# Cross-attention in two layers on one core: projections as four column tiles side by side

## The chip, the cores and the metric

One NeuronCore of a Trainium2 chip. The metric is the device time of one execution in microseconds. The engines named below are PE (TensorE: matrix products, with its loads of the stationary operand shown apart as PEld), DVE (VectorE), ACT (ScalarE), POOL (GpSimd) and SP (SyncE, which here only issues DMAs).

## The reference

Two cross-attention layers follow each other on x (32 sequences of 256 tokens, 320 channels) with one context (32 sequences of 77 tokens, 512 channels), 20 heads of 16 channels. With this context of 77 tokens the parts of the reference for other kinds of context are empty, and each layer comes to this:

```python
q = heads(x @ Wq); k = heads(ctx @ Wk); v = heads(ctx @ Wv)
p = softmax(q @ k.T / sqrt(16))
x = merge(p @ v) @ Wo + bo + x
```

Layer 0 makes x for layer 1; both read the same context, so keys and values of both layers can be made at any time. All numbers are fp32.

## The kernel before

Activations are kept with channels on partitions. Sequences go in pairs (NB = 2, 16 pairs), and a *unit* is one pair in one layer, 32 in all, ordered so that layer 0 runs AHEAD = 4 pairs in front of layer 1. The 320 channels are split into two full parts of 128 rows and a rest of 64; the rests of both sequences of a pair share one tile of 128 rows, so a unit has NG = 5 groups of 128 channel rows by 256 tokens: g = 0 to 3 are (part, sequence), g = 4 holds both rests. Every group is eight heads.

The steps of a unit, with what each runs on PE (stationary rows x columns, then elements streamed):

- keys_rest (L225): the last 64 key channels of both sequences, four tiles of 128x32 side by side, 77 elements, four steps of the contraction. keys (L242): the two full parts for both sequences at once, one tile of 128x128, 154 elements, four steps each.
- queries (L266, through project) and queries_rest (L275, through project_rest).
- project (L175) is used for Q and for the output. For parts t = 0, 1, contraction blocks kc = 0, 1 and sequences b = 0, 1 it runs a 128x128 tile over 256 tokens (L195). The last 64 input channels are a 64-row contraction (last_channels, L184): sequence 0 lies in rows 0 to 63 and sequence 1 in rows 64 to 127, each a tile of 64x128. Where last_channels stands is set by rest: before part 0 (rest = 0), between the parts (1), or at the end (2). Queries use u % 2, the output 0, the last unit 2.
- project_rest (L213): the last 64 output channels, four tiles of 128x32, three contraction steps.
- vals (L290): values for a chunk of 128 context tokens of a layer (not of a pair; 20 chunks a layer, the last of 32 tokens): tokens are the columns of the stationary operand, 128x128, and 320 elements are streamed.
- maxima (L326): four tiles of 32x128; DVE takes the maxima over keys (L334). turn (L343) transposes them, and eight small DMAs (L347) put them into rows of the queries.
- scores (L360): four tiles of 32x77, eight products for each group; ACT takes exp (L366).
- values (L409): products (L380), four tiles of 77x32 side by side; then DVE, POOL and DVE divide and transpose.
- finish (L430, project on the output weights) and finish_rest (L438); DVE adds bias and residual (L421).

All results of PE go through one pool of eight PSUM banks, one tag. The order of every engine's work is written out by hand (manual_schedule): each group of each unit has a slot, slots run one after another, and in a slot steps are issued in the order load, maxima, turn, scores, values, rest, full, last (L497). "rest" holds keys_rest, queries_rest and finish_rest; "full" holds keys and vals; "last" holds queries and finish. Values of two groups are made in every second slot. So nearly every slot on PE is maxima, then scores, then perhaps values, then one of the projection steps. Loads come on SP's queue.

Of the kernel before, what the change touches and what calls it, by code (L numbers as in the profile page):

```python
# [86 lines left out]
def xattn_kernel(ctx: ExitStack, tc: tile.TileContext, xT, cT, cP, weights, outT):  # L90
    nc = tc.nc
# [10 lines left out]
    def bank(name):  # L102
        return psum.tile([P, 512], F32, tag="bank", name=name)
# [45 lines left out]
    for i in range(2):  # L149
        m = const.tile([P, 2 * NG, 32], F32, name=f"max_{i}")  # L150
# [15 lines left out]

    st = [{} for _ in units]

    def of_group(x, g):

        if g < 4:
            return x[:, (g // 2) * NT + (g % 2) * S : (g // 2) * NT + (g % 2 + 1) * S]
        return x[:, 2 * NT : NX]

    def project(ps, w, w2, x, rest=0):  # L175

        def last_channels():  # L180
            for t in range(2):
                for b in range(NB):
                    r = slice(64 * b, 64 * b + 64)
                    nc.tensor.matmul(  # L184
                        ps[t][b][:, 0:S], w2[r, 0, t * P : (t + 1) * P], x[r, 2 * NT : NX],
                        start=(t >= rest), stop=(t < rest),
                    )

        for t in range(2):
            if t == rest:  # L190
                last_channels()
            for kc in range(2):
                for b in range(NB):
                    i = kc * NT + b * S
                    nc.tensor.matmul(  # L195
                        ps[t][b][:, 0:S], w[:, kc, t * P : (t + 1) * P], x[:, i : i + S],
                        start=(kc == 0 and t < rest), stop=(kc == 1 and t >= rest),
                    )
        if rest == 2:
            last_channels()  # L200
# [34 lines left out]
    def keys(u):  # L235
        p, layer = units[u]
        w, c_sb = w_sb[layer], cs[u]
        kT = st[u]["k"]
        for t in range(2):
            ps = bank(f"psk_{u}_{t}")  # L240
            for kc in range(NKA):
                nc.tensor.matmul(  # L242
                    ps[:, 0 : 2 * L],
                    w["k"][:, kc, t * P : (t + 1) * P],
                    c_sb[:, kc, :],
                    start=(kc == 0),
                    stop=(kc == NKA - 1),
                )
            nc.vector.tensor_tensor(  # L249
                kT[:, :, 2 * t : 2 * t + 2].rearrange("p e g k -> p e (g k)"),  # L250
                ps[:, 0 : 2 * L].unsqueeze(1).broadcast_to([P, 2, 2 * L]),
                masks.unsqueeze(2).broadcast_to([P, 2, 2 * L]),
                ALU.mult,
            )
        kM = st[u]["km"] = work.tile([P, 2, NG, L], F32, tag="kM", name=f"kM_{u}", bufs=3)
        for e in range(2):
            nc.gpsimd.tensor_scalar_add(kM[:, e], kT[:, e], less[:, e : e + 1])  # L257

    def queries(u):
        p, layer = units[u]  # L260
        w = w_sb[layer]
        q0, _ = st[u]["q"] = [
            work.tile([P, NX], F32, tag=f"q{e}", name=f"q{e}_{u}", bufs=3) for e in range(2)
        ]
        ps = [[bank(f"psq_{u}_{t}_{b}") for b in range(NB)] for t in range(2)]
        project(ps, w["q"], w["q2"], xs[p], rest=u % 2)  # L266
        for g in range(4):
            nc.scalar.copy(of_group(q0, g), ps[g // 2][g % 2][:, 0:S])  # L268

    def queries_rest(u):  # L270
        p, layer = units[u]
        w = w_sb[layer]
        q0, q1 = st[u]["q"]
        ps = bank(f"psq_{u}_2")
        project_rest(ps, w["q"], w["q22"], xs[p])  # L275
        nc.scalar.copy(of_group(q0, 4), ps[:, 0:S])
        nc.sync.dma_start(out=q1, in_=q0)
# [6 lines left out]
    def vals(layer, i):  # L284

        n = min(P, B * L - i * P)
        stage, c_sb = stages[layer][i % 2], cvs.pop((layer, i))
        ps = bank(f"psv_{layer}_{i}")
        for kc in range(NKA):
            nc.tensor.matmul(  # L290
                ps[:n, :C],
                c_sb[:, kc, :n],
                w_sb[layer]["v"][:, kc, :],
                start=(kc == 0),
                stop=(kc == NKA - 1),
            )
        nc.scalar.copy(
            stage[:n].rearrange("p r e a d -> p r (e a) d")[:, :, 0:4:3, :],
            ps[:n, :C].rearrange("p (r e d) -> p r e d", e=2, d=HD),
        )  # L300
# [18 lines left out]
    def maxima(u, g):  # L319
        q0, kT, mx = st[u]["q"][0], st[u]["k"], maxes[u % 2]  # L320
        q = of_group(q0, g)
        ps = [bank(f"psm_{u}_{g}_{j}") for j in range(4)]
        for c in range(S // P):
            for j in range(4):
                r = slice(32 * j, 32 * j + 32)
                nc.tensor.matmul(  # L326
                    ps[j][:, c * 2 * L : (c + 1) * 2 * L],
                    q[r, c * P : (c + 1) * P],
                    kT[r, :, g, :],
                    start=True,  # L330
                    stop=True,
                )
        for j in range(4):
            nc.vector.tensor_reduce(  # L334
                mx[:, 2 * g : 2 * g + 2, 2 * j : 2 * j + 2],
                ps[j][:, : 4 * L].rearrange("p (c e k) -> p c e k", e=2, k=L),
                AX.X,
                ALU.max,
            )
# [87 lines left out]
    def finish(u):  # L427
        w = w_sb[units[u][1]]
        ps = [[bank(f"psy_{u}_{t}_{b}") for b in range(NB)] for t in range(2)]
        project(ps, w["o"], w["o2"], st[u]["o"], rest=2 if u == NU - 1 else 0)  # L430
        for g in range(4):
            add(u, g, ps[g // 2][g % 2])
# [18 lines left out]
    for u, (p, layer) in enumerate(units):  # L451
# [5 lines left out]
        if u > 0:  # L457
            at(s - 12, "load", lambda u=u: load_context(u))
        at(s - 8 if odd else s - 9, "rest", lambda u=u: keys_rest(u))
        at(s - 7 if odd else s - 8 if u else s - 9, "full", lambda u=u: keys(u))  # L460
        at(s - 9, "last", lambda u=u: queries(u))
        need = range(p * NB * L // P, ((p + 1) * NB * L - 1) // P + 1)
        new = [i for i in need if i >= made[layer]]
        for i in need:
            when = s - 5 if odd else s - 6
            if len(new) == 2:
                when = s - 6 if i < new[1] else s - 5
            if i in new:
                at(when - 3, "load", lambda layer=layer, i=i: load_chunk(layer, i))
                at(when, "full", lambda layer=layer, i=i: vals(layer, i))  # L470
                made[layer] += 1
            at(when, "full", lambda u=u, i=i: place_vals(u, i))
# [124 lines left out]
```

## Time and profile before

| quantity | value |
|---|---|
| median of the 3 runs shown | 1009.54 us |
| all three | 1003.88, 1009.54, 1009.67 us |
| the profiled execution: its own time | 1003.92 us |
| the profiled execution: its span | 1002.1 us |
| granted TensorE clock, mean | 1.0 |

The page gives each group of instructions with its busy time and the mean of one. The groups on PE that matter here, with the tile (stationary rows * columns) and the elements streamed:

```profile
L360 PE MATMUL pss<-q,kM 32*77 32x256 f32 x2560 | 171.3, 375 | 1.9 <-DMA q<-mT 1.9
L380 PE MATMUL po<-pT,v 77*32 77x256 f32 x2560 | 155.9, 382 | 0.0
L195 PE MATMUL psq<-x,w 128*128 128x256 f32 x512 | 123.3, 389 | 0.0
L195 PE MATMUL psy<-oT,w 128*128 128x256 f32 x512 | 119.1, 386 | 0.0
L242 PE MATMUL psk<-c,w 128*128 128x154 f32 x512 | 77.6, 305 | 0.0
```

Each line has the program's line, the engine, the tile written and those read, the shape, the number of records, the busy time and the mean length of one record (ns), and the time that PE was idle just ahead of such records. A product of fp32 operands shows as two records, each with a load of its own. Matmuls are pipelined and their ends are modelled, so records overlap in the list. The order of time (timeline) lists blocks of like records by their start; the chain of waits follows the work that ended last back to its cause.

### The profile page before, as it was taken

What the parts mean: (1) busy time and instruction counts of PE and PEld (TensorE: products, weight loads), DVE (VectorE), ACT (ScalarE), POOL (GpSimd) and SP (SyncE); (2) the same over time, 40 slices, a digit from 0 to 9 for tenths busy, and PEclk for the clock granted to TensorE, in tenths of its full rate; (3) what the DMA queues carried; (4) which work ended last, traced back from release to release, by engine and by line L of the source; (5) the groups of instructions that cost most, each with busy time, mean ns of one, the idle gap of its engine ahead of it and who ended that gap; (6) DMA issues with size and microseconds to landing.
All of it is one profiled execution on the core that took longest, in us unless ns stands there. A gap on an engine that the chain in (4) does not pass through costs nothing.

```text
span 1002.1 us, 29771 instructions
## 1 busy us (share of the span) xinstructions
PE 989.1 (99%) x12608; PEld 695.4 (69%) x12608; DVE 587.9 (59%) x1380; ACT 420.7 (42%) x905; POOL 183.0 (18%) x236
## 2 busy tenths in 40 slices
PE   7999999999999999999999999999999999999998
PEld 5666776667776767767677676677666776676755
DVE  2456655566665666555666555665656666566664
ACT  1354434444444434444444444443543444443453
POOL 2111102111120111101111021111201112011111
PEclk9999999999999999999999999999999999999999
DMA  5541222221132311323113132121322212230012
GB/s 207 185 150 40 77 69 95 68 75 66 52 121 68 109 52 42 120 78 118 37 60 101 64 121 69 68 74 58 122 78 72 69 44 94 68 104 30 24 71 80
DMA packets 53894, 82.69 MB, mean 83 GB/s; under 512 B 15556, under 2 KB 35652, under 8 KB 53762
## 3 DMA queue, kind: packets, MB, share of 16 engines
q1 hardware_dynamic: 53330, 78.96, 23.7%
q8 instruction: 99, 1.62, 0.6%
q10 hardware_dynamic: 432, 1.84, 0.5%
q14 instruction: 33, 0.27, 0.1%
HBM read 35.39 MB, written 10.49 MB: 46 GB/s over the span
## 4 chain that ended last, share of the span: by engine, by line
PE 97%; DVE 1%; DMA 1%; SPq 0%; POOL 0%; issue 0%; POOLq 0%
PE po L380 15%; PE pss L360 14%; PE psq L195 12%; PE psy L195 12%; PE psm L326 12%; PE psv L290 9%; PE psk L242 7%; PE psy L213 4%; PE psq L213 4%; PE psy L184 3%; PE psq L184 3%; PE psk L225 2%; DVE max L334 1%; DMA w<-in_w_dram 0%; SPq L347 0%; DVE turned L392 0%
## 5 line engine op out<-in xcount | busy, mean ns | idle before, releaser
L366 ACT ACTIVATE pT<-pss 77x512 f32<-77x512 f32 x640 | 327.1, 592 | 357.8 <-PE pss L360 357.8
L334 DVE TENSOR_REDUCE max<-psm 128x4 f32<-128x308 f32 x640 | 261.4, 471 | 267.6 <-PE psm L326 267.6
L401 POOL TENSOR_TENSOR normal<-turned,inv 128x256 f32<-128x256 f32 x160 | 99.4, 621 | 542.0 <-DVE inv L396 542.0
L360 PE MATMUL pss<-q,kM 32*77 32x256 f32 x2560 | 171.3, 375 | 1.9 <-DMA q<-mT 1.9
L380 PE MATMUL po<-pT,v 77*32 77x256 f32 x2560 | 155.9, 382 | 0.0
L326 PE MATMUL psm<-kT,q 32*128 32x154 f32 x2560 | 130.4, 314 | 1.3 <-DVE max L334 0.8
L326 PEld LDWEIGHTS psm<-kT,q 32*128 32x128 f32 x2560 | 92.9, 183 | 55.8 <-issue 52.6
L257 POOL TENSOR_SCALAR kM<-kT,less 128x385 f32<-128x385 f32 x64 | 80.0, 1263 | 268.9 <-DVE kT L249 268.9
L380 PEld LDWEIGHTS po<-pT,v 77*32 77x32 f32 x2560 | 75.3, 109 | 71.7 <-DVE max L334 28.8
L392 DVE STREAM_TRANSPOSE turned<-po 128x512 f32<-128x512 f32 x160 | 109.5, 684 | 24.3 <-PE po L380 24.3
L195 PE MATMUL psq<-x,w 128*128 128x256 f32 x512 | 123.3, 389 | 0.0
L360 PEld LDWEIGHTS pss<-q,kM 32*77 32x77 f32 x2560 | 109.1, 141 | 15.4 <-issue 3.2
L195 PE MATMUL psy<-oT,w 128*128 128x256 f32 x512 | 119.1, 386 | 0.0
L195 PEld LDWEIGHTS psq<-x,w 128*128 128x128 f32 x512 | 93.3, 190 | 27.1 <-issue 10.8
L195 PEld LDWEIGHTS psy<-oT,w 128*128 128x128 f32 x512 | 94.6, 190 | 22.3 <-issue 10.3
L421 DVE SCALAR_TENSOR_TENSOR x<-psy,w,x 128x256 f32<-128x256 f32 x160 | 72.7, 476 | 43.9 <-PE psy L195 40.7
L290 PE MATMUL psv<-w,cv 128*128 128x320 f32 (+1 forms) x320 | 96.7, 445 | 0.8 <-DVE max L334 0.8
L414 DVE STREAM_TRANSPOSE oT<-normal 128x256 f32<-128x256 f32 x160 | 71.1, 445 | 34.4 <-POOL normal L401 34.4
L290 PEld LDWEIGHTS psv<-w,cv 128*128 128x128 f32 (+1 forms) x320 | 56.2, 185 | 35.9 <-DVE max L334 12.5
L268 ACT COPY q<-psq 128x256 f32<-128x256 f32 x128 | 46.1, 373 | 82.8 <-PE psq L195 70.2
L242 PEld LDWEIGHTS psk<-c,w 128*128 128x128 f32 x512 | 70.2, 193 | 11.6 <-DVE max L334 11.4
L242 PE MATMUL psk<-c,w 128*128 128x154 f32 x512 | 77.6, 305 | 0.0
(28 smaller groups left out, 446.3 us busy)
## 6 DMA issues: line engine op xcount, KB each, us to landing
q<-q SPq DMA_DIRECT2D x32, 640.0 KB
x<-in_xT_dram SPq DMA_DIRECT2D x16, 640.0 KB
c<-in_cP_dram SPq DMA_DIRECT2D x32, 308.0 KB
cv<-in_cT_dram SPq DMA_DIRECT2D x38, 256.0 KB
out_dram<-x SPq DMA_DIRECT2D x15, 640.0 KB
v<-stage SPq DMA_DIRECT2D x26, 192.5 KB
q<-mT SPq DMA_DIRECT2D x256, 5.0 KB
w<-in_w_dram ACTq DMA_DIRECT2D x2, 640.0 KB
```

What stands on the lines that cost most here:

```text
L195: nc.tensor.matmul(ps[t][b][:, 0:S], w[:, kc, t * P : (t + 1) * P], x[:, i : i + S], start=(kc == 0 and t < rest), stop=(kc == 1 and t >= ...
L213: nc.tensor.matmul(ps[r, 0:S], lhsT, rhs, start=(kc == 0), stop=(kc == 2))
L242: nc.tensor.matmul(ps[:, 0 : 2 * L], w["k"][:, kc, t * P : (t + 1) * P], c_sb[:, kc, :], start=(kc == 0), stop=(kc == NKA - 1),)
L257: nc.gpsimd.tensor_scalar_add(kM[:, e], kT[:, e], less[:, e : e + 1])
L290: nc.tensor.matmul(ps[:n, :C], c_sb[:, kc, :n], w_sb[layer]["v"][:, kc, :], start=(kc == 0), stop=(kc == NKA - 1),)
L326: nc.tensor.matmul(ps[j][:, c * 2 * L : (c + 1) * 2 * L], q[r, c * P : (c + 1) * P], kT[r, :, g, :], start=True, stop=True,)
L334: nc.vector.tensor_reduce(mx[:, 2 * g : 2 * g + 2, 2 * j : 2 * j + 2], ps[j][:, : 4 * L].rearrange("p (c e k) -> p c e k", e=2, k=L), AX.X ...
L360: nc.tensor.matmul(ps[j][:L, e * S : (e + 1) * S], kM[r, e, g, :], q[r, :], start=True, stop=True,)
L366: nc.scalar.activation(st[u]["p", g][j][:L], ps[j][:L], AF.Exp, scale=SCALE)
L380: nc.tensor.matmul(po[32 * j : 32 * j + 32, e * S : (e + 1) * S], vpad[:L, b, pair, e].rearrange("p a d -> p (a d)"), pT[j][:L, e * S : (e ...
L392: nc.vector.transpose(turned[:, 0 : 2 * S], po)
L401: nc.gpsimd.tensor_tensor(normal.rearrange("p q e d -> p e q d"), outs, inv.unsqueeze(3).broadcast_to([P, 2, S // 32, HD]), ALU.mult,)
```

## The change

A helper by_columns cuts a product's output into slices of 32 rows and issues one product for each, with the same streamed operand and 32 columns of the stationary one. It is put in place of the single product at four places: the 64-row part of project (L184), the 128-row part of project (L195), keys (L242) and vals (L290). A 128x128 tile becomes four tiles of 128x32 side by side, the form that products and project_rest have; the pair of 64x128 tiles becomes eight tiles of 64x32. Slots, the order of steps, tiles and DMAs are as before. Lines below the helper move down by six.

```diff
@@ -166,6 +167,11 @@
 
     st = [{} for _ in units]
 
+    def by_columns(out, lhsT, rhs, **flags):
+
+        for m in range(0, out.shape[0], 32):
+            nc.tensor.matmul(out[m : m + 32], lhsT[:, m : m + 32], rhs, **flags)
+
     def of_group(x, g):
 
         if g < 4:
@@ -181,7 +187,7 @@
             for t in range(2):
                 for b in range(NB):
                     r = slice(64 * b, 64 * b + 64)
-                    nc.tensor.matmul(
+                    by_columns(
                         ps[t][b][:, 0:S], w2[r, 0, t * P : (t + 1) * P], x[r, 2 * NT : NX],
                         start=(t >= rest), stop=(t < rest),
                     )
@@ -192,7 +198,7 @@
             for kc in range(2):
                 for b in range(NB):
                     i = kc * NT + b * S
-                    nc.tensor.matmul(
+                    by_columns(
                         ps[t][b][:, 0:S], w[:, kc, t * P : (t + 1) * P], x[:, i : i + S],
                         start=(kc == 0 and t < rest), stop=(kc == 1 and t >= rest),
                     )
@@ -239,7 +245,7 @@
         for t in range(2):
             ps = bank(f"psk_{u}_{t}")
             for kc in range(NKA):
-                nc.tensor.matmul(
+                by_columns(
                     ps[:, 0 : 2 * L],
                     w["k"][:, kc, t * P : (t + 1) * P],
                     c_sb[:, kc, :],
@@ -287,7 +293,7 @@
         stage, c_sb = stages[layer][i % 2], cvs.pop((layer, i))
         ps = bank(f"psv_{layer}_{i}")
         for kc in range(NKA):
-            nc.tensor.matmul(
+            by_columns(
                 ps[:n, :C],
                 c_sb[:, kc, :n],
                 w_sb[layer]["v"][:, kc, :],
```

## The prediction

> **What bounds the kernel now.** I read the page first: busy shares, then the chain that ended last, then the waits of PE, then the order of time of PE in a steady stretch.
>
> ```profile
> span 1002.1 us, 29771 instructions
> PE 989.1 (99%) x12608; PEld 695.4 (69%) x12608; DVE 587.9 (59%) x1380; ACT 420.7 (42%) x905; POOL 183.0 (18%) x236
> PE 97%; DVE 1%; DMA 1%; SPq 0%; POOL 0%; issue 0%; POOLq 0%
> ```
>
> ```profile
> PE psk L225 <- DMA w<-in_w_dram: 5.7, 1, 5.7
> PE pss L360 <- DMA q<-mT: 1.9, 2, 1.6
> ```
>
> PE is busy all the time, the chain runs through PE for 97% of the span, and the waits of PE for others come to some 10 us, 5.7 of them at the start. So a nanosecond saved on PE is a nanosecond saved, and the question is what PE's time consists of. The order of time shows it (first column: start; second: first start to last modelled end, so I use the distance to the next line's start instead):
>
> ```profile
> 500.04 1.99 PE L195 MATMUL psq<-x,w 128*128 128x256 f32 x8
> 501.96 1.14 PE L184 MATMUL psq<-x,w 64*128 64x256 f32 x8
> 503.03 1.99 PE L195 MATMUL psq<-x,w 128*128 128x256 f32 x8
> 504.95 0.81 PE L326 MATMUL psm<-kT,q 32*128 32x154 f32 x16
> 505.58 1.04 PE L360 MATMUL pss<-q,kM 32*77 32x256 f32 x16
> 506.55 1.93 PE L380 MATMUL po<-pT,v 77*32 77x256 f32 x32
> 508.31 0.72 PE L225 MATMUL psk<-c,w 128*32 128x77 f32 x32
> 508.95 1.13 PE L184 MATMUL psy<-oT,w 64*128 64x256 f32 x8
> 510.02 3.72 PE L195 MATMUL psy<-oT,w 128*128 128x256 f32 x16
> 513.67 0.81 PE L326 MATMUL psm<-kT,q 32*128 32x154 f32 x16
> 514.30 1.10 PE L360 MATMUL pss<-q,kM 32*77 32x256 f32 x16
> 515.33 2.37 PE L242 MATMUL psk<-c,w 128*128 128x154 f32 x16
> 517.63 0.81 PE L326 MATMUL psm<-kT,q 32*128 32x154 f32 x16
> ...
> 521.03 1.48 PE L213 MATMUL psy<-oT,w 128*32 128x256 f32 x24
> 522.33 1.48 PE L213 MATMUL psq<-x,w 128*32 128x256 f32 x24
> 523.74 0.81 PE L326 MATMUL psm<-kT,q 32*128 32x154 f32 x16
> 524.37 1.04 PE L360 MATMUL pss<-q,kM 32*77 32x256 f32 x16
> 525.34 2.42 PE L290 MATMUL psv<-w,cv 128*128 128x320 f32 x8
> 527.69 0.81 PE L326 MATMUL psm<-kT,q 32*128 32x154 f32 x16
> ```
>
> Every fp32 product is two records, so L195's 16 records are eight products.
>
> **A pass costs the same in both forms.** L195 takes 3.65 us for 16 records and 1.92 for 8: 1.73/8 = 0.216 us a record, plus 0.19 a block. L213 takes 1.30 for 24 records of four tiles side by side: 6 passes of 0.217, plus nothing, because the next block has the same form. Four tiles of 32 columns thus stream 256 elements as fast as one tile of 128 columns. L225 (77 elements) takes 0.64 - 0.11 (below) = 0.53 for 8 passes, 0.066 each, so four loads and four products can be issued every 0.066 us; the slimmest pass that the change makes has 154 elements. The change gains nothing inside a block. (The page's "mean ns of one" and busy time hide this, since each block's modelled tail is counted in.)
>
> **What is paid at a change of form.** L213 before another L213 takes 1.30, before L326 1.41: leaving a four-tile form costs 0.11. L380, entered from L360 and followed by L225 of its own form, takes 1.76 for 8 passes, 8 x 0.216 + 0.03: entering costs 0.03. A block of 128 columns pays 0.19 to 0.20 for both together (L195 0.19; L184 1.07 - 4 x 0.216 = 0.21; L242 and L290 likewise).
>
> **What the Trainium skill says.** *TensorEngine Tiling (Array Packing)*, Tiling Modes, Key Properties: changing the tiling mode, not just the tile, drains TensorE. The trace agrees, at 0.09 to 0.11 a change. L326 to L360 (0.63) shows no drain: 32x77 counts as 32x128. *TensorE: Matmul & The Clock Gate*, LDWEIGHTS (loading the stationary operand): a load takes about columns/1.2 ns and rows don't matter, so an estimate of 107 ns for 128 columns and 27 for 32. That is the entry: after a drain the load for the second record of a product lies open. The 0.03 of L380 agrees with 27; 0.19 splits into 0.107 entry and 0.09 exit; with L242's pass, (2.30 - 0.20)/16 = 0.131, L326's 0.63 is 4 x 0.131 + 0.107. The same page, Part 3, The mechanism, says that tiles at different positions overlap. The trace shows four columns (L380), four rows (L326) and two halves of 64 rows (L184), but no mix of rows and columns. *Perfetto Trace Analysis*, Identifying the Most-Contended Engine, warns that matmul busy share is a poor measure; here its 99% contains the drains.
>
> **The sum.** PE's steps keep their slots and order; DVE, ACT and POOL and all DMAs stay as they are, none is moved past another, and no wait is added. PE gets 3 x (1024 + 512 + 512 + 304) = 7056 more products and as many loads (psq/psy of 256 elements, 64-row parts, psk, psv in chunks of 128 tokens), 12608 to 19664, hidden under the passes as L225 shows. Instruction fetch grows by the same instructions: 1.62 MB at 0.6% of the DMA engines to about 2.5 MB; I cost it at nothing, since L225's burst is already as dense.
>
> I counted form changes in time order. Before, 463: into 128 columns 77 from pss, 63 from a 64-row part, 46 from four columns into a 64-row part, 18 from 128 rows into one, 10 from four columns into 128 (214 in all); 87 into four columns; 162 into psm. After, in the changed program's order, 452: 162 into psm, 162 from pss into four columns, and each of the 64 projections goes once into its 64-row part and once out.
>
> - Entries: before 214 x 0.107 + 87 x 0.027 = 25.2 us; after (162 + 64 + 64) x 0.027 = 7.8. **-17.4.** psm's 162 are unchanged.
> - Exits: starts of side-by-side tiles are 7 ns apart, so a drain ends later after four tiles: 0.113, against 0.093 after one tile and 0.100 after a pair; eight tiles, by the same step, 0.14. Before 87 x 0.113 + 150 x 0.093 + 64 x 0.100 = 30.2; after 226 x 0.113 + 64 x 0.14 = 34.5. **+4.3.**
>
> Sum **-13.1 us**, all of it on PE's path. The profiled execution took 1003.92 us, 1.8 more than its span; it becomes 990.8. The median of the runs shown is 1009.54, 5.6 above this execution, so the same sum there gives 996.4. One run of three lay low, two high; weighted so, (990.8 + 2 x 996.4)/3, that is **995 us**.
>
> Not shown by this trace: the eight tiles of 64x32. Their entry could be 0.107 instead of 0.027 (+5 us), if the row halves' loads queue; I take 0.027, because L326's four row tiles load together. The form change between 64 and 128 rows could cost nothing (-20 us); L195 to L184 to L195 at 500 us, where only rows differ, pays it both times, which excludes that. Overlap is bounded below by 4 passes a part, above by 8.
>
> **Rivals.**
> 1. *The two row halves of the 64-row parts run behind each other*, because products are issued half by half (b outer, columns inner). Serial: 4 more passes of 0.216 in 64 parts, +55 us, net +42: 1037 to 1046, **slower**. It decides from 0.20 us a part (no gain left) and makes over 1% from (13.1 + 10)/64 = 0.36, under two passes. Against: L184's halves and L380's columns run together. For: no mixed form is in the trace.
> 2. *The second half lags by one pass only*: 64 x 0.216 = +13.8, net +0.7: **no change**, 1005 to 1010.
> 3. *A wait takes the gain back*: with shorter slots the rows q<-mT land too late for pss. Now that is 1.9 us in two of 32 units. From the last of a unit's eight issues to its first pss most units have 3.1 to 5.8 us, and two with 2.1 did not wait; a slot shrinks by at most 0.3. If 16 units lost that, +5: net -8, 996 to 1001, **within 1%**. DVE at 59% and the eight banks show only 0.8 us of wait at psm.
> 4. *The four tiles don't stream at full pace here* (four reads of one x instead of two or four different ones): 1840 passes of 256, 154 or 320 elements change form, so 7 ns a pass cancels the gain and 12.4 makes it slower by over 1%. Against: L213 reads one x with two tiles at 0.217.
> That the change doesn't do what it says is excluded for the count of tiles, not for their overlap: that is rivals 1 and 2.
>
> **How the numbers follow.** Forecast 0.66, rival 2 0.09, rival 3 0.08, rivals 1 and 4 together 0.17. About 1% is what a measurement can tell here (the runs themselves spread 0.6%). The forecast is -1.3%, so of its 0.66 I give 0.56 to faster and 0.10 to within 1%; rival 3 adds 0.02 and 0.06, rival 2 0.09, the slow ones 0.16 and 0.01. Faster 0.58, same 0.26, slower 0.16. The range goes from 986 (the low runs, a little more gain) to 1009, which takes in rivals 2 and 3; what lies above is left out.
>
> **What would show it.** Start to next start: psk in 128 rows by 32 columns after pss 2.24 us (2.30 before), psv 2.29 (2.35), 0.14 less where a four-column block stands ahead; the psy block before psm 3.60 (3.65); a 64-row part 1.03 (1.07 before) with 64 records; L213's successor of the same form right behind it. A 64-row part of 1.25 or 1.9 us is rival 2 or 1; passes above 0.22 rival 4; a new line of PE waiting for q<-mT rival 3. The prediction is wrong if the number of form changes or the price of an entry is not what I read.

## The result, and the profile after

| | before | changed |
|---|---|---|
| median of all runs shown at first | 1006.79 us (1003.88 to 1009.67, 4 runs) | 993.64 us (992.67 to 994.41, 4 runs) |
| ratio, 95% interval | | 0.987 [0.983, 0.991] |
| profiled execution, own time and span | 1003.92, 1002.1 us | 994.41, 992.6 us |
| repeated (last experiment): median | 1004.11 us (11 runs) | 994.17 us (6 runs) |
| ratio, 95% interval | | 0.990 [0.987, 0.993] |

The change is a gain of 1.0 to 1.3%. The forecast was 995 us with a range of 986 to 1009. The two ratios differ with the share of runs of the kernel before that took 2 to 6 us longer; where the granted TensorE clock is on record, it averaged 0.993 to 0.998 over those and 1.0 over the others. With both kernels at a clock of 1.0 the repeated series has medians of 1003.7 and 993.4: **10.3 us** (1.0%) belong to the change. The profiled executions, both at 1.0, differ by 9.5.

The page after, its totals and the summary of the chain of waits:

```profile
span 992.6 us, 43883 instructions
PE 979.3 (99%) x19664; PEld 601.0 (61%) x19664; DVE 588.0 (59%) x1380; ACT 420.7 (42%) x905; POOL 183.1 (18%) x236
PE 97%; DVE 1%; DMA 1%; SPq 0%; POOL 0%; issue 0%; ACT 0%; POOLq 0%
```

PE has the 19664 records that the prediction counted, and is still the bound. The other engines do the same work as before. The order of time on PE, in a stretch like that of the prediction (start, first start to last modelled end, instruction):

```profile
494.79 4.82 PE L173 MATMUL psq<-x,w 128*32 128x256 f32 x96
499.54 0.81 PE L332 MATMUL psm<-kT,q 32*128 32x154 f32 x16
500.17 1.04 PE L366 MATMUL pss<-q,kM 32*77 32x256 f32 x16
501.14 1.93 PE L386 MATMUL po<-pT,v 77*32 77x256 f32 x32
502.89 0.72 PE L231 MATMUL psk<-c,w 128*32 128x77 f32 x32
503.55 4.68 PE L173 MATMUL psy<-oT,w 64*32 64x256 f32 x96
508.16 0.81 PE L332 MATMUL psm<-kT,q 32*128 32x154 f32 x16
508.79 1.13 PE L366 MATMUL pss<-q,kM 32*77 32x256 f32 x16
509.85 2.31 PE L173 MATMUL psk<-c,w 128*32 128x154 f32 x64
512.09 0.81 PE L332 MATMUL psm<-kT,q 32*128 32x154 f32 x16
512.72 1.12 PE L366 MATMUL pss<-q,kM 32*77 32x256 f32 x16
513.77 1.93 PE L386 MATMUL po<-pT,v 77*32 77x256 f32 x32
...
518.86 1.04 PE L366 MATMUL pss<-q,kM 32*77 32x256 f32 x16
519.83 2.36 PE L173 MATMUL psv<-w,cv 128*32 128x320 f32 x32
522.12 0.81 PE L332 MATMUL psm<-kT,q 32*128 32x154 f32 x16
522.75 1.07 PE L366 MATMUL pss<-q,kM 32*77 32x256 f32 x16
523.75 1.93 PE L386 MATMUL po<-pT,v 77*32 77x256 f32 x32
```

Read from start to next start: psk takes 2.24 us (before 2.30), psv 2.29 (2.35), the query projection with its 64-row part in the middle 4.75 (before 1.92 + 1.07 + 1.92 = 4.91), the output projection 4.61 (1.07 + 3.65 = 4.72). But pss (L366) has grown where the slot before it ended with such a block: 1.06 us after psy and 1.05 after psk (in the kernel before 1.03 and 1.03), 1.00 after psv (0.97). Summed over all blocks of the two traces, start to next start: projections -7.5 us, keys and values in 128 rows -4.4, the short blocks of L219 and L231 -1.1, together **-13.0**; pss **+3.5**. What is left, -9.5, is the difference of the spans. Of the 3.5 us, 0.7 are one single wait at 765.7 us, where ACT's copy of a values chunk began 0.85 us after psm's start in place of 0.13. Why it was late is not shown. In the trace of the repeated run (last experiment) that wait is missing and pss has grown by 2.8.

### The profile page after: what moved, and what is told of

The parts are those of the page before. It is cut to its first block, busy times and chain, and to the rows that moved or that the text cites. A ratio compares the mean times of both kernels' runs of the same rounds, so it can differ in the third digit from the quotient of the medians.

```text
span 992.6 us, 43883 instructions
## 1 busy us (share of the span) xinstructions
PE 979.3 (99%) x19664; PEld 601.0 (61%) x19664; DVE 588.0 (59%) x1380; ACT 420.7 (42%) x905; POOL 183.1 (18%) x236
## 4 chain that ended last, share of the span: by engine, by line
PE 97%; DVE 1%; DMA 1%; SPq 0%; POOL 0%; issue 0%; ACT 0%; POOLq 0%
PE psq L173 15%; PE psy L173 15%; PE po L386 15%; PE pss L366 14%; PE psm L332 12%; PE psv L173 9%; PE psk L173 7%; PE psy L219 4%; PE psq L219 4%; PE psk L231 2%; DVE max L340 1%; DMA c<-in_cP_dram 1%; SPq L353 0%; DVE turned L398 0%; DMA q<-mT 0%; POOL normal L407 0%
## 5 line engine op out<-in xcount | busy, mean ns | idle before, releaser
L366 PE MATMUL pss<-q,kM 32*77 32x256 f32 x2560 | 174.7, 376 | 1.9 <-DMA q<-mT 1.8
L173 PE MATMUL psq<-x,w 128*32 128x256 f32 (+1 forms) x3072 | 152.1, 382 | 0.0
L173 PE MATMUL psy<-oT,w 128*32 128x256 f32 (+1 forms) x3072 | 149.9, 381 | 0.0
L366 PEld LDWEIGHTS pss<-q,kM 32*77 32x77 f32 x2560 | 114.1, 141 | 13.9 <-issue 3.2
L173 PEld LDWEIGHTS psq<-x,w 128*32 128x32 f32 (+1 forms) x3072 | 77.3, 108 | 67.2 <-issue 20.2
L173 PEld LDWEIGHTS psy<-oT,w 128*32 128x32 f32 (+1 forms) x3072 | 79.0, 108 | 64.1 <-issue 19.3
L173 PE MATMUL psv<-w,cv 128*32 128x320 f32 x1232 | 94.2, 435 | 0.8 <-DVE max L340 0.8
L173 PE MATMUL psk<-c,w 128*32 128x154 f32 x2048 | 75.6, 300 | 0.0
L173 PEld LDWEIGHTS psk<-c,w 128*32 128x32 f32 x2048 | 64.6, 111 | 12.5 <-DVE max L340 11.4
L173 PEld LDWEIGHTS psv<-w,cv 128*32 128x32 f32 x1232 | 38.1, 110 | 47.6 <-DVE max L340 12.1
```

What stands on the lines that cost most here:

```text
L173: nc.tensor.matmul(out[m : m + 32], lhsT[:, m : m + 32], rhs, **flags)
L366: nc.tensor.matmul(ps[j][:L, e * S : (e + 1) * S], kM[r, e, g, :], q[r, :], start=True, stop=True,)
```

## The experiments

Three theories were put to the test. *Theory A*: PE pays by the form change, and most of the gain is the load that lies open on entry (estimated in the prediction at 107 ns for 128 columns and 27 for 32). *Theory R*, its rival: what is saved is drains, because the projections now have the form of their neighbours. *Theory B*: the growth of pss is a wait for a bank that is evacuated (read out by ACT or DVE) later than before.

**Keys and values alone.** In both parts of project the single product is put back.

```diff
-                    by_columns(
+                    nc.tensor.matmul(
                         ps[t][b][:, 0:S], w2[r, 0, t * P : (t + 1) * P], x[r, 2 * NT : NX],
...
-                    by_columns(
+                    nc.tensor.matmul(
                         ps[t][b][:, 0:S], w[:, kc, t * P : (t + 1) * P], x[:, i : i + S],
```

> Keys and values as four tiles of 32 columns, both parts of project as in the kernel before. Theory A (what is saved is the load that lies open after a drain: 107 ns for 128 columns, 27 for 32): the psk and psv blocks that follow pss take 2.24 and 2.29 us to the next start (2.30 and 2.35 before), the psv blocks that follow L219 about 2.27, in all 5.4 us of PE time less than before. 2.0 us come back (30 + 38 blocks x 0.03), since evacuation starts 0.03 us later after four tiles and pss waits for that bank. Net -3.4 us, ratio 0.997, span about 998.7. Theory R (what is saved is drains, by having the form of the neighbours): only the nine form changes that vanish count, at 0.2 us each, -1.8 us, and blocks between pss and psm stay at 2.30 and 2.35.

Measured: 1000.5 us, ratio 0.994 [0.992, 0.996]; at clock 1.0 1000.5 against 1003.9, -3.4. (Its profiled execution had a clock of 0.997 and a span of 1001.4.) In its trace psk takes 2.24 and psv 2.29. The -3.4 is what theory A said; theory R said -1.8 and unchanged blocks.

**Project alone.** The opposite: keys (L242) and vals (L290) as before.

```diff
-                by_columns(
+                nc.tensor.matmul(
                     ps[:, 0 : 2 * L],
...
-            by_columns(
+            nc.tensor.matmul(
                 ps[:n, :C],
```

> Both parts of project in 32-column tiles, keys and values as in the kernel before. Theory A: -7.6 us of form changes (from 214 entries at 107 ns to entries at 27, dearer exits), 0.9 us back as a bank wait after the 29 psy blocks (0.03 each): net -6.7, ratio 0.993, span about 995.4. With the run of keys and values it adds up to the whole change (-3.4 - 6.7 = -10.1; the profiled executions show -9.5). Theory R: only two form changes vanish (464 to 462), so about -0.4 us.

Measured: 997.5 us, ratio 0.991 [0.987, 0.994], span 995.8; at clock 1.0 -6.5, where theory A said -6.7 and theory R -0.4. The two halves add up to -9.9 of the 10.3.

**The 64-row parts alone.** by_columns is kept at L184 only, so that eight tiles of 64x32 stand among 128x128 ones.

```diff
-                    by_columns(
+                    nc.tensor.matmul(
                         ps[t][b][:, 0:S], w[:, kc, t * P : (t + 1) * P], x[:, i : i + S],
```

The single product stands in keys and vals too.

> The 64-row parts alone as eight tiles of 64x32, everything else in 128 columns. Theory A: the entry into a 64-row part falls from 107 to 27 ns and its exit rises from 0.100 to 0.14 us: 1.07 to 1.03 us a part, 64 parts, -2.5 us, no bank wait more (blocks ahead of psm end in one tile), ratio 0.9975, span 999.6. Theory R: the number of form changes stays 464, so no gain, or a loss since 64x32 is one more form: 0 to +3. Rival 1 of the prediction (halves behind each other): 1.9 us a part, +50 us; the trace of the whole change already shows 1.02 for it.

Measured: 1001.7 us, ratio 0.995 [0.993, 0.997], span 999.8; at clock 1.0 -2.3. The order of time of this run on PE:

```profile
500.98 1.09 PE L173 MATMUL psq<-x,w 64*32 64x256 f32 x32
502.00 2.00 PE L201 MATMUL psq<-x,w 128*128 128x256 f32 x8
503.93 0.81 PE L332 MATMUL psm<-kT,q 32*128 32x154 f32 x16
```

The 64-row part takes 1.02 us: four passes of 0.216, one entry, one exit. So eight tiles in two rows and four columns run all at once. The block of 128 columns behind it still pays 1.93. Here the number of form changes is the same as before and one more form is in use, and still it gains: against theory R.

**Tiles of 64 columns.**

```diff
-        for m in range(0, out.shape[0], 32):
-            nc.tensor.matmul(out[m : m + 32], lhsT[:, m : m + 32], rhs, **flags)
+        for m in range(0, out.shape[0], 64):
+            n = min(m + 64, out.shape[0])
+            nc.tensor.matmul(out[m:n], lhsT[:, m:n], rhs, **flags)
```

> The whole change with tiles of 64 columns instead of 32: two of 128x64, four of 64x64. The form is then not that of products and project_rest, so form changes are as many as before (464). Theory A: an entry costs 64 columns' load, 53 ns, so PE's form changes come to 9.6 us less than before (3.4 more than with 32 columns): psk between pss and psm about 2.25 us, a 64-row part about 1.03; with 0 to 3 us of bank waits span 992.5 to 995.5, ratio about 0.991 to 0.993. Theory R (sharing the form of the neighbours is what counts): nothing of the gain is left, span about 1002.

Measured: 996.1 us, ratio 0.989 [0.985, 0.994]; its two runs at clock 1.0 took 995.6 and 995.8, -8.2. (The profiled execution had 0.995.) On PE:

```profile
509.06 1.11 PE L367 MATMUL pss<-q,kM 32*77 32x256 f32 x16
510.10 2.32 PE L174 MATMUL psk<-c,w 128*64 128x154 f32 x32
512.36 0.81 PE L333 MATMUL psm<-kT,q 32*128 32x154 f32 x16
```

psk takes 2.26. The form is shared with no neighbour, and four fifths of the gain are there. Theory R falls: it is the open load that shrank. The Trainium skill (*TensorE: Matmul & The Clock Gate*, LDWEIGHTS (loading the stationary operand)) gives about columns/1.2 ns for a load, an estimate of 53 ns for 64 columns; in this trace the step from the first to the second record of a tile after an entry is 51 to 52 ns longer than the steps that follow. The same reading gives 104 ns for 128 columns in the kernel before and 24 for 32 columns in the changed one.

**The copy of values in two instructions.** It doubles what theory B suspects.

```diff
-        nc.scalar.copy(
-            stage[:n].rearrange("p r e a d -> p r (e a) d")[:, :, 0:4:3, :],
-            ps[:n, :C].rearrange("p (r e d) -> p r e d", e=2, d=HD),
-        )
+        for h in range(2):
+            r = slice(h * HEADS // 4, (h + 1) * HEADS // 4)
+            nc.scalar.copy(
+                stage[:n].rearrange("p r e a d -> p r (e a) d")[:, r, 0:4:3, :],
+                ps[:n, :C].rearrange("p (r e d) -> p r e d", e=2, d=HD)[:, r],
+            )
```

> The whole change, with the copy of a values chunk out of its PSUM bank made in two instructions of 160 elements instead of one of 320. Theory B (pss waits for the bank that was evacuated last): a copy takes 0.43 us for 320 elements and 0.37 for 256, so about 0.29 for 160, two take 0.15 us longer than one, and the pss block after a values chunk grows from 1.00 to about 1.15 us, 38 times: +5.7 us on PE, span about 998. Rival (the 0.03 us have another cause, as PE's own form change): pss blocks stay at 1.00, span 992.6.

Measured: span 998.6 at clock 0.995, so the time says little, but the blocks do. First the timeline of the changed kernel, then of this one (chosen lines):

```profile
522.12 0.81 PE L332 MATMUL psm<-kT,q 32*128 32x154 f32 x16
522.25 0.43 ACT L303 COPY stage<-psv 128x320 f32<-128x320 f32 x1 [0.23 <-PE psv L173]
522.62 0.75 PEld L366 LDWEIGHTS pss<-q,kM 32*77 32x77 f32 x16
522.75 1.07 PE L366 MATMUL pss<-q,kM 32*77 32x256 f32 x16
```

```profile
522.93 0.81 PE L334 MATMUL psm<-kT,q 32*128 32x154 f32 x16
523.07 0.49 ACT L305 COPY stage<-psv 128x160 f32<-128x160 f32 x2 [0.24 <-PE psv L173]
523.43 0.81 PEld L368 LDWEIGHTS pss<-q,kM 32*77 32x77 f32 x16
523.56 1.13 PE L368 MATMUL pss<-q,kM 32*77 32x256 f32 x16
```

The two copies end 0.06 us later (0.49 against 0.43), not the 0.15 that I had put, and pss goes from 1.00 to 1.06 us to its next start. Its excess over a pss block that waits for nothing (0.97) is 0.090 in place of 0.030, in nearly every one of the 38 cases, so it follows the end of the copies. The same rule fits every trace: the excess is the end of the evacuation, counted from psm's start, less 0.53 us. Before, the end and the excess are 0.533 and 0 for psv, 0.588 and 0.057 for psk, 0.592 and 0.062 for psy; after, 0.563 and 0.029, 0.617 and 0.085, 0.622 and 0.092. The copies of the queries end at 0.48 before and 0.51 after, and the pss block behind them has no excess. The starts of the single records say which tile waits: behind psk and psy those of the first three tiles are as in a block without a wait, and the fourth tile's last one comes 721 to 727 ns into the block in place of 665 (before), 752 to 757 (after). Theory B is shown. The fourth tile of pss takes the bank that was allotted eight banks earlier, which is the one that ACT or DVE reads last. The list of waits doesn't show it, since PE is busy with the other three tiles.

**Sequence outside, contraction inside, in project.**

```diff
-            for kc in range(2):
-                for b in range(NB):
+            for b in range(NB):
+                for kc in range(2):
```

> The whole change, with the sequence loop outside the contraction loop in the 128-row part of project, so that sequence 0's bank is done four records of passes ahead of sequence 1's instead of two. Theory B: the last residual add no longer stands behind the one before it on DVE (it now starts 0.478 us after the last matmul, and would start at 0.448), so the pss block after psy falls from 1.06 to 1.03 us, 29 times: -0.9 us. Form changes are as they were. Rival: no change of pss after psy.

Measured: 993.6 us (one run), span 991.8, and pss after psy as in the changed kernel, 0.092 over. I was wrong on DVE: the last residual add was not held up by the one before it. It ends 0.62 us after psm's start in both orders.

**The 64-row part first in all query projections**, with the order of the run above.

```diff
-        project(ps, w["q"], w["q2"], xs[p], rest=u % 2)
+        project(ps, w["q"], w["q2"], xs[p], rest=0)
```

> As the run before, and the 64-row part of every query projection at its start (in odd units it lies between the two parts now). Theory A: 16 form changes fewer (453 to 437), each an exit of 0.113 and an entry of 0.027, -2.2 us; with -0.9 us from theory B, -3.1 us to the whole change: span about 989, time about 990.5 at full clock, ratio to the kernel before about 0.984 to 0.987. Rival: the 64-row part's place costs nothing or is paid by a later evacuation of the queries: no change, 993.6.

Measured: 999.5 us, ratio 0.993 [0.990, 0.995]; at clock 1.0 998.5, so 5 us *more* than the changed kernel in place of 3 less. The timeline of an odd unit (chosen lines):

```profile
494.74 0.81 PE L332 MATMUL psm<-kT,q 32*128 32x154 f32 x16
495.37 1.04 PE L366 MATMUL pss<-q,kM 32*77 32x256 f32 x16
495.57 1.64 DVE L340 TENSOR_REDUCE max<-psm 128x4 f32<-128x308 f32 x4 [0.66 <-PE psm L332]
496.34 5.14 PE L173 MATMUL psq<-x,w 64*32 64x256 f32 x96
501.41 0.81 PE L332 MATMUL psm<-kT,q 32*128 32x154 f32 x16
```

The projection takes 5.07 us against 4.75. Its 64-row part needs all four banks at once. They are those of psm, eight allotments ago, and DVE reads the last of them until 497.21, 0.87 us after the block has begun. With rest = 1 part 0 runs first and needs two banks only. The waits of PE's loads agree: psq for DVE's maxima 12.5 us in 45 cases against 5.6 in 15. This block saves one form change (0.14) and loses 0.46 to the wait.

**Columns outside, contraction inside, in keys and values.**

```diff
-            for kc in range(NKA):
-                by_columns(
-                    ps[:, 0 : 2 * L],
...
+            for m in range(0, P, 32):
+                for kc in range(NKA):
+                    nc.tensor.matmul(
+                        ps[m : m + 32, 0 : 2 * L],
+                        w["k"][:, kc, t * P + m : t * P + m + 32],
```

vals likewise.

> The whole change, but keys and values issue all contraction steps of one column tile before the next tile (columns outside, contraction inside), so that eight records of one tile stand ahead of the next tile's first. Theory W (PE looks far enough ahead to fill the other tiles): psk blocks stay at 2.24 us and psv blocks at 2.29, no change of time. Theory S (PE issues in order, and a tile holds only a few records): the tiles run one behind another, a part of keys takes up to 29 passes of 0.131 instead of 8 and a chunk of values up to 29 of 0.269 instead of 8, at most +176 us and +215 us; anything between tells how many records a tile holds. The 64-row parts, where two records a tile stand ahead of the next, are not touched.

Measured: 1204.0 us, span 1202.2. On PE:

```profile
582.61 5.14 PE L249 MATMUL psk<-c,w 128*32 128x154 f32 x64
587.68 0.81 PE L334 MATMUL psm<-kT,q 32*128 32x154 f32 x16
...
597.50 5.66 PE L298 MATMUL psv<-w,cv 128*32 128x320 f32 x32
603.10 0.81 PE L334 MATMUL psm<-kT,q 32*128 32x154 f32 x16
```

psk takes 5.07 us, psv 5.60. A psv chunk is 8 passes with all tiles at once and 32 one behind another; (5.60 - 0.14)/0.269 is 20, and the starts show why: each tile's first record starts with the *fifth* of the tile before it (0, then 1.107, 2.213 and 3.320 us into a block). Three tiles that come four passes late each make 8 + 3 x 4. The psk blocks agree: seven delays of 0.555 and eight passes of 0.131 make 5.07 with the same 0.14. So one tile had about four records under way or waiting at a time, and the next tile's first came through only when the fifth began. It starts at 1.107 us, ahead of the sixth (1.370), though the program has it behind the eighth. PE does look past records that wait, but not far, and both theories were half right.

**The changed kernel once more.** The kernel is the changed one, without an edit.

> The changed kernel once more, against the kernel before. Theory C (the ratio 0.987 holds more than PE's saving: half of the runs of the kernel before had a granted clock of 0.993 to 0.998 and lie 2 to 6 us higher): runs of both at clock 1.0 differ by 10.4 us (1003.9 and 993.5), 3.4 less than the 13.1 of form changes, the part that comes back as bank waits; some runs of the changed kernel show a lower clock too and then lie 2 to 6 us above 993.5. Rival (the change itself keeps the clock up): no run of the changed kernel shows a clock under 1.0, while half of those of the kernel before do.

Measured: 994.2 us, ratio 0.990 [0.987, 0.993], span 991.3. At clock 1.0 four runs of the changed kernel took 992.8 to 994.6 and seven of the kernel before 1003.4 to 1004.2. Two of six runs of the changed kernel had a clock of 0.997 and took 997.3 and 998.3, so the rival falls: the spell of a lower clock comes to both. Theory C's 10.4 us came out as 10.3.

## Why the prediction was right, and where it was off

- *A pass costs the same in both forms*: right. After the change passes of 256 elements still start 0.216 us apart, those of 154 0.131, those of 320 0.269, with four times the instructions. The page alone, with its mean lengths and busy times, could not tell this; the starts could.
- *Entries -17.4, exits +4.3, sum -13.1*: right, and term by term. The blocks concerned gave -13.0, and the blocks that the prediction named came at 2.24, 2.29, 4.61 (forecast 1.03 + 3.60) and 1.02 us. Read from the starts of the records, an entry is 104 ns for 128 columns and 24 for 32 (put at 107 and 27, so the 80 ns between them hold), and an exit 0.093 us after one tile, 0.097 after a pair, 0.113 after four, 0.137 after eight; between blocks of the same form both are nothing. The 64-column run shows that entries follow the number of columns, not the likeness to the neighbours.
- *Eight tiles at once, entry 27 ns*: right, and it was the main thing that the trace before could not show. The fear behind rivals 1 and 2, that the order of issue keeps tiles apart, is real: with eight records of one tile ahead of the next in keys and values, the kernel took 210 us longer. The changed kernel puts two.
- *"No wait is added"*: this is the step that failed. The prediction took the list of waits for the whole and put DVE and the banks down as covered. pss did wait, 0.06 us in each of 59 blocks, before the change already. After it, evacuation starts 0.03 us later and 97 blocks wait 0.03 longer: 2.9 us, and the single wait of 0.7 makes it 3.5 in the profiled execution. The forecast -13.1 and +2.8, the growth of pss in the repeated run, make the -10.3 us measured at a clock of 1.0. Rival 3 had the right kind of case, a wait that takes a part of the gain back, but named q<-mT, which stayed at 1.8 us in two cases.
- *The time*: 990.8 was forecast for an execution like the profiled one; it took 994.4, and 3.5 of the 3.6 are those waits. The 995 us came near 993.6 also because I had raised it for the two high runs of the kernel before. That was luck: the reason was wrong. Those runs go with a lower clock in the single execution, and the four first runs of the changed kernel had none.
- *Two sums*: rival 1 should read 1046 to 1052 us in place of 1037 to 1046: 1037 is 995 + 42, and 995 already has the gain of 13.1 in it, so the whole 55 come on top; and in rival 4 it is 12.6 ns a pass, not 12.4. Neither bears on the forecast.

No version that I ran is clearly faster than the changed kernel.

## What to carry to other kernels

Where PE is the bound with short blocks of many forms, count the form changes and price each as an exit (0.09 to 0.14 us here) plus the load that lies open (0.104, 0.051 and 0.024 us here for 128, 64 and 32 columns). Narrower tiles side by side stream as fast here and enter cheaper. Issue the tiles in turn (two records each here), not one tile's whole contraction first. A gain on PE can be taken back in part by whoever empties the banks. Look at the blocks that come one ring of banks later: here the wait of one tile of four stood in no list of waits.

## What the runs showed of the hardware

- From the last matmul's start to the start of the evacuation that waits for it: psv 0.469 us for one tile of 128 columns, 0.480 for two of 64, 0.499 for four of 32; psk 0.329, 0.339, 0.359. That is about 10 ns for each further tile. In the run with columns outside, where the last passes had one tile of 32 alone, it was 0.469 and 0.329 again, so it goes by tiles that run together, not by their width. The Trainium skill (*TensorE: Matmul & The Clock Gate*, Part 3, The cost: per-tile semaphore tail) fits the time behind a packed group with 4.7 ns a tile; here it is twice that.
- The lower clock, where a trace has it, is a spell at half speed. In the profiled execution of the 64-column run (busy time of each engine, then the granted clock, by stretches in us):

```profile
940.00:950.00 10.00, 10.00 (x160) 5.53 (x152) 6.35 (x16) 4.88 (x12) 1.32 (x3) 1.00 0.48 174
950.00:955.00 5.00, 4.19 (x62) 3.02 (x58) 3.88 (x11) 2.63 (x6) 1.24 (x2) 0.97 0.01 3
955.00:960.00 5.00, 5.00 (x49) 2.22 (x42) 2.92 (x7) 2.04 (x4) 0.00 (x0) 0.50 0.02 3
960.00:965.00 5.00, 5.00 (x38) 2.34 (x32) 1.72 (x4) 0.00 (x0) 1.24 (x2) 0.51 0.04 8
965.00:970.00 5.00, 5.00 (x73) 2.97 (x71) 1.83 (x4) 1.63 (x4) 0.00 (x0) 1.00 0.00 0
```

PE is idle for 0.8 us between 950 and 955, waiting for DVE's maxima near the end of the work, and then runs at a clock of 0.5 for some ten microseconds. The run with two copies has the same spell, and the run with the 64-row part first a shorter one. The Trainium skill (same page, Part 1, What's actually happening) tells of a clock gate that goes to half speed after an idle window of about 3.4 us; here the stretch shows only 0.8 us of idle time ahead of the spell. The profiled executions before and after have that idle time too and no spell, so it is not shown to be the cause. That this spell accounts for every high run of the kernel before is likely from their clocks (0.993 to 0.998) but not shown: no trace of such a run was taken.
